# Two attention and expert layers: a head group's products with v issued in one go, filler pieces placed by estimated durations

## The chip, the cores and the metric

One NeuronCore of one Trainium2 chip runs the whole kernel in one launch. The metric is the device time of one execution in microseconds (us); lower is better. Three runs of the kernel before took 1697.82, 1705.48 and 1710.2 us, median 1705.48.

The engines named below are TensorE's matmuls (PE) and weight loads (PEld), VectorE (DVE), ScalarE (ACT), GpSimd (POOL) and SyncE (SP, which issues DMAs). Each engine executes its own instructions in order and waits for others by semaphores.

## The reference

Eight sequences of 512 tokens, 256 wide, pass through two blocks of attention and mixture of experts, all in float32:

```python
x = x + attention0(layernorm(x))   # 16 heads of 16, 4 kv heads, rotary, causal
x = x + ffn0(layernorm(x))         # 32 experts, inner 96, top 8, weights renormalised
x = x + attention1(layernorm(x))   # 16 heads of 16, causal
x = x + ffn1(layernorm(x))         # 16 experts, inner 176, top 2, and a shared FFN of inner 352
```

Attention is `softmax(q k^T / 4) v` under a causal mask, then an output projection. The FFNs are `(silu(x w1) * (x w3)) w2`, weighted by the router's softmax.

## The kernel before

The span has four large stages: attention of layer 0 with routing (30 to 393 us), experts of layer 0 (422 to 884), attention of layer 1 with routing and shared FFN (884 to 1410), experts of layer 1 (1420 to 1657). The change touches the two attention stages.

**One sequence, one group.** `Attention.steps(b)` walks over four head groups c of four heads each. The scores of a group are made transposed, keys on partitions, in three sets n: keys 0 to 127 against all 512 queries (512 wide); keys 128 to 255 and 384 to 511 (384 and 128 wide); keys 256 to 383 (256 wide). `scores` (L638) makes a set as one matmul per head and key block, 32 rows of the array per head, into the PSUM tile `st` (four banks, one buffer). One ACT instruction (L643) takes the exp of a set into `probs`; DVE multiplies the diagonal blocks by the causal mask (L649, 128x512 each, four a group).

`values` (L661) multiplies by v: four key blocks (512, 384, 128, 256 wide) of four heads each, accumulated in the PSUM tile `o` (one bank), 32 output columns of the array per head, with a column of ones that gives the softmax sum. Then DVE copies o to `osb` (L667), PE transposes it (L674, `ot`), and DVE divides by the sum (L677, L678) into `otok`.

**Filler.** `values` is a generator of six pieces. `steps` yields twice per score set, 24 times a sequence, and takes one piece of the preceding group's `values` before each yield. At each yield `pipeline` (L734) also takes pieces of two other generators: `before(b+1)`, which is the norm (`xn_a`), its transposes (`xT_a`, L308) and the q, k and v projections of the next sequence; and `finish(b-1)`, which is the output projection (`oT`, L719; `y`, L727) and `after`, that is the FFN norm (`xn_f`, L292), its transposes (`xT_f`, L308), the router's logits (L321), the choice of experts and the ranks (DVE, and `rk`, L368 and L370), scatters of the rows to DRAM by POOL (L385) and, in layer 1, the shared FFN (`sg`, `su`, L402; silu on ACT, L406; `sy`, L415). Pieces are counted, not weighed: made in equal steps over the sequence, `finish(b-1)` by step 22 of 24 in layer 0 and by the end of the sequence in layer 1. In layer 1 the third generator, `ahead1(b+3)`, gathers a later sequence's x from the experts' outputs (L1200, POOL), from the first step on.

**What sets the order.** The code's order gives priorities; the framework's scheduler then fixes each engine's order from them, from dependencies and from its own cost model. So a piece can be moved away from where the code has it, and a set of four matmuls can be separated by other matmuls. PSUM tiles of all filler pieces come from one ring of three banks (`bank`). `xn_f` has two buffers in layer 0 and one in layer 1; the x tiles form a ring of five.

Of the kernel before, what the change touches and what calls it, by code (L numbers as in the profile page):

```python
# [12 lines left out]
ALU = mybir.AluOpType  # L13
# [59 lines left out]
STEPS = 2 * len(BANKS)  # L73
# [17 lines left out]
def two_blocks_kernel(  # L91
# [78 lines left out]
    def biases1(tmp, bank):  # L170
        wide = tmp.tile([P, ND, P], F32, tag="wide", name="wide", bufs=1)
        lo, _ = BB["o"]
        for m in range(ND):
            nc.vector.tensor_copy(wide[:, m, :], bias1[:, lo + m : lo + m + 1].to_broadcast([P, P]))
        tr = bank("ob")
        for m in range(ND):
            nc.tensor.transpose(tr[:, m * P : (m + 1) * P], wide[:, m, :], ident)
        nc.scalar.copy(ob.rearrange("p m d -> p (m d)"), tr[:, : ND * P])
        yield

        lower = tmp.tile([P, P], F32, tag="lower", name="lower", bufs=1)
        nc.vector.memset(lower[:, :DH], 0.0)
        nc.vector.tensor_copy(lower[:, DH:], ident[:, : P - DH])
        upper_half = tmp.tile([P, 2, 2, 2], F32, tag="upper_half", name="upper_half", bufs=1)
        for n, which in enumerate("qk"):
            lo, hi = BB[which]
            nc.vector.tensor_scalar(
                upper_half[:, :, n, :], bias1[:, lo:hi].rearrange("p (m s) -> p s m", s=2), half[:, 0:1], None, ALU.mult
            )
        both = bank("qkb")[:, :4]  # L190
        for s, turn in enumerate((ident, lower)):
            nc.tensor.matmul(
                both, turn, upper_half[:, s, :, :].rearrange("p n m -> p (n m)"), start=(s == 0), stop=(s == 1)
            )
        nc.vector.tensor_copy(qkb.rearrange("p n m -> p (n m)"), both)
        for s in range(2):
            nc.vector.tensor_scalar(kb[:, :, s], qkb[:, 1, :], half[:, s : s + 1], None, ALU.mult)
        yield
# [98 lines left out]
    def free():  # L297

        for _ in range(4):
            yield  # L300

    def turned(xn, lnp, bank, name):

        xT = lnp.tile([P, ND, T], F32, tag="xT", name=f"xT_{name}")
        for c in range(ND):
            tr = bank(f"xT_{name}_{c}")
            for t in range(NT):
                nc.tensor.transpose(tr[:, t * P : (t + 1) * P], xn[:, t, c * P : (c + 1) * P], ident)  # L308
            nc.scalar.copy(xT[:, c, :], tr)
            yield  # L310
        return xT

    def ffn_parts(smp, bank):
        def route(n, b, xn, xT, name, again):
# [10 lines left out]
            yield  # L325
# [11 lines left out]
            yield  # L337
# [10 lines left out]
            yield  # L348
# [15 lines left out]
            yield  # L364
# [26 lines left out]
            yield  # L391

        def shared(w, xT, x, name):

            hs = smp.tile([P, NS, T], F32, tag="hs", name=f"hs_{name}", bufs=1)
            for n in range(NS):
                rows = min(P, IS1 - n * P)
                g, u = bank(f"sg_{name}_{n}"), bank(f"su_{name}_{n}")
                for o, base in ((g, 0), (u, ND * P)):
                    for c in range(ND):  # L400
                        at = base + c * P
                        nc.tensor.matmul(  # L402
                            o[:rows, :], w[:, n, at : at + rows], xT[:, c, :], start=(c == 0), stop=(c == ND - 1)
                        )
                h = hs[:rows, n, :]
                nc.scalar.activation(h, g[:rows, :], AF.Silu)  # L406
                nc.vector.tensor_tensor(h, h, u[:rows, :], ALU.mult)
                yield
            for half_ in range(NT // 2):
                y = bank(f"sy_{name}_{half_}").rearrange("p (t d) -> p t d", t=2)  # L410
                for i in range(2):
                    t = 2 * half_ + i
                    for n in range(NS):
                        rows = min(P, IS1 - n * P)
                        nc.tensor.matmul(  # L415
                            y[:, i, :], hs[:rows, n, t * P : (t + 1) * P], w[:rows, n, 2 * ND * P :],
                            start=(n == 0), stop=(n == NS - 1),
                        )
                xh = x[:, 2 * half_ : 2 * half_ + 2, :]
                nc.vector.tensor_tensor(xh, xh, y, ALU.add)  # L420
                yield
# [193 lines left out]
    class Attention:  # L615
# [6 lines left out]
        def __init__(self, n, late, ptp, ps, bank, wo, masked=None):  # L622
            self.n, self.fine, self.late, self.ptp, self.ps, self.bank, self.wo = n, fines[n], late, ptp, ps, bank, wo
            self.heads, self.otok, self.rec = {}, {}, {}
            self.last = iter(())
            self.masked = masked

        def scores(self, b, c, n, probs):
# [13 lines left out]
            pt = self.ptp.tile([P, NG, width], F32, tag="p2" if n == 2 else "p01", name=f"p_{name}", bufs=1 + (n < 2))  # L642
# [10 lines left out]
        def values(self, b, c, probs):  # L653
# [4 lines left out]
            for step, j in enumerate((0, 1, 3, 2)):  # L658
# [6 lines left out]
                yield  # L665
            osb = late.tile([P, T], F32, tag="osb", name=f"osb_{name}", bufs=1)
            nc.vector.tensor_copy(osb, o)  # L667
            yield
# [4 lines left out]
            for t in range(NT):  # L673
                nc.tensor.transpose(ot[:, t * P : (t + 1) * P], osb[:, t * P : (t + 1) * P], ident)  # L674
# [7 lines left out]
            yield  # L682

        def steps(self, b):

            for c in range(NCK):  # L690
                probs = {}
                for n in range(len(BANKS)):
                    self.scores(b, c, n, probs)
                    next(self.last, None)
                    yield
                    if n == len(BANKS) - 1:
                        self.last = self.values(b, c, probs)
                    next(self.last, None)
                    yield
                    self.mask(n, probs)  # L700

        def flush(self):
            for _ in range(STEPS - 1):
                next(self.last, None)
                yield

        def output(self, b, x):
# [8 lines left out]
            for k in range(ND):  # L716
# [4 lines left out]
                yield  # L721
            for h in range(NT // 2):
# [9 lines left out]
                yield  # L732

    def pipeline(att, before, after, n_before, n_after, till, ahead=None, lead=0):  # L734
# [9 lines left out]
        n_steps = NCK * STEPS  # L744
        n_after += 4
        drain(before(0))
        for b in range(NB):
            pre = before(b + 1) if b + 1 < NB else iter(())
            post = finish(b - 1) if b else iter(())
            early = ahead(b + 3) if ahead and b + 3 < NB else iter(())  # L750
            made_pre = made_post = 0
            for n, _ in enumerate(att.steps(b)):
                while made_post < n_after * (n + 1 - STEPS) // (till - STEPS):
                    next(post, None)
                    made_post += 1
                while made_pre < n_before * (n + 1 - lead) // (n_steps - 2 - lead):
                    next(pre, None)
                    made_pre += 1
                next(early, None)
            drain(pre)  # L760
            drain(post)
            drain(early)
        drain(att.flush())
        drain(finish(NB - 1))
# [24 lines left out]
    def fast0(awp, lnp, atp, late, ptp, ps, bank):  # L789
# [38 lines left out]
        def before(b):  # L828
# [11 lines left out]
            for t in range(NT):  # L840
# [27 lines left out]
                yield  # L868
            qT = atp.tile([P, 2, T], F32, tag="qT", name=f"qT_{name}")
            for m in range(2):  # L870
# [4 lines left out]
                yield  # L875
# [9 lines left out]
            yield  # L885
# [36 lines left out]
    def fast1(w, v1s, lnp, atp, late, ptp, ps, bank, last):  # L922
# [3 lines left out]
        def before(b):  # L926
# [9 lines left out]
            for h in range(NT // 2):  # L936
# [11 lines left out]
                yield  # L948
            qT = atp.tile([P, 2, T], F32, tag="qT", name=f"qT_{name}")
            kT = atp.tile([P, 2, 2, T], F32, tag="kT", name=f"kT_{name}")  # L950
            for m in range(2):
# [3 lines left out]
                nc.vector.tensor_scalar(qT[:, m, :], q, qkb[:, 0, m : m + 1], None, ALU.add)  # L955
                yield
                kk = bank(f"k_{name}_{m}")
                for k in range(ND):
                    nc.tensor.matmul(kk, w["k"][:, k, m, :], xn[:, k, :], start=(k == 0), stop=(k == ND - 1))
                nc.scalar.activation(  # L960
                    kT[:, m, 0, :], kk, AF.Identity, bias=kb[:, m, 0:1], scale=half[:, 0:1]
                )
                nc.vector.tensor_scalar(
                    kT[:, m, 1, :], kk, half[:, 1:2], kb[:, m, 1:2], ALU.mult, ALU.add
                )
                yield
            att.heads[b] = lambda c: (qT[:, c // 2, :], kT[:, c // 2, c % 2, :], v1, c * NG * (DH + 1))
# [3 lines left out]
    def tables(lay, small, bank, again, beside=None):  # L971
# [10 lines left out]
        yield  # L982
# [10 lines left out]
        yield  # L993
# [4 lines left out]
        yield  # L998
# [5 lines left out]
        yield  # L1004
# [4 lines left out]
        yield  # L1009
# [12 lines left out]
        yield  # L1022

        for lo in range(0, n_e, 8):
# [10 lines left out]
            yield  # L1035
# [206 lines left out]
    def load_x(b, tmp, bank, xf=None):  # L1242
# [3 lines left out]
        for h in range(NT // 2):  # L1246
# [6 lines left out]
            yield  # L1253
# [126 lines left out]
    with ExitStack() as s:  # L1380
# [21 lines left out]
        pipeline(att, before, after0, 15, 12, 22)  # L1402


    with ExitStack() as s1:
# [4 lines left out]
        with ExitStack() as s:  # L1410
# [15 lines left out]
            def after1(b):  # L1426
# [4 lines left out]
                yield from route(1, b, xn, xT, name, False)  # L1431
                yield from shared(w1["s"], xT, xs[b], name)
# [5 lines left out]
            pipeline(att, before, after1, 15, 17, NCK * STEPS, ahead1, 4)  # L1438
# [246 lines left out]
```

## Time and profile before

| | us |
|---|---|
| median of three runs | 1705.48 |
| profiled execution | 1701.29 |
| its span | 1699.6 |
| mean granted TensorE clock | 0.961 |

Starts of the first score set of sequences 0 to 7 in the trace: 30.7, 73.5, 120.0, 164.8, 212.4, 257.8, 307.7, 351.5 in layer 0, and 884.5, 933.1, 996.1, 1059.1, 1122.2, 1191.1, 1261.9, 1324.9 in layer 1.

Three lines of the costliest groups of the page show how it is read: line, engine, operation, tiles and count; then busy time and the mean of one in ns; then the engine's idle time before them and what ended it.

```profile
L638 PE MATMUL st_a<-qT_a,kT_a 32*128 32x512 f32 (+3 forms) x2048 | 202.1, 478 | 11.1 <-ACT p_a L643 10.8
L649 DVE TENSOR_TENSOR p_a<-p_a,causal 128x512 f32<-128x512 f32 x256 | 170.8, 686 | 57.3 <-ACT p_a L643 56.1
L661 PE MATMUL o_a<-p_a,v 128*32 128x512 f32 (+3 forms) x2048 | 197.4, 455 | 6.9 <-DVE p_a L649 6.7
```

A float32 matmul leaves two records, so x2048 are 1024 matmuls: 16 for each of the 64 head groups (8 sequences, 4 groups, 2 layers), four heads in each of four widths. Matmuls of the four heads of a set run side by side in the array, so their busy times overlap, and the distance between starts is the better measure of what a set costs.

### The profile page before, as it was taken

What the parts mean: (1) busy time and instruction counts of PE and PEld (TensorE: products, weight loads), DVE (VectorE), ACT (ScalarE), POOL (GpSimd) and SP (SyncE); (2) the same over time, 40 slices, a digit from 0 to 9 for tenths busy, and PEclk for the clock granted to TensorE, in tenths of its full rate; (3) what the DMA queues carried; (4) which work ended last, traced back from release to release, by engine and by line L of the source; (5) the groups of instructions that cost most, each with busy time, mean ns of one, the idle gap of its engine ahead of it and who ended that gap; (6) DMA issues with size and microseconds to landing.
All of it is one profiled execution on the core that took longest, in us unless ns stands there. A gap on an engine that the chain in (4) does not pass through costs nothing. (4 is left out here: it accounts for less than half of the span.)

```text
span 1699.6 us, 30922 instructions
## 1 busy us (share of the span) xinstructions
PE 1543.7 (91%) x10180; PEld 1029.0 (61%) x10180; DVE 992.0 (58%) x3131; ACT 650.7 (38%) x865; POOL 792.1 (47%) x660
## 2 busy tenths in 40 slices
PE   5899999995999999999989999999899988999982
PEld 2455454543898999998853454544444545777761
DVE  5678887875555555555455764764656544444452
ACT  2555554552233333333334554454355331222221
POOL 0017677577710004888888448888511011000473
PEclk9999999997999999999999999999899998999996
DMA  2035557236988778999995245664312024343563
GB/s 73 13 87 156 163 167 270 102 139 207 307 256 269 202 201 226 266 264 273 268 194 71 39 107 80 127 136 72 86 52 79 26 84 159 109 159 116 156 225 120
DMA packets 255128, 259.43 MB, mean 153 GB/s; under 512 B 80212, under 2 KB 235988, under 8 KB 254964
## 3 DMA queue, kind: packets, MB, share of 16 engines
q1 hardware_dynamic: 199172, 167.88, 32.5%
q0 software_dynamic: 55296, 88.65, 23.0%
q8 instruction: 87, 1.43, 0.4%
q10 hardware_dynamic: 496, 0.85, 0.1%
q14 instruction: 77, 0.63, 0.1%
HBM read 132.70 MB, written 124.57 MB: 151 GB/s over the span
## 5 line engine op out<-in xcount | busy, mean ns | idle before, releaser
L1200 POOL DMA_INDIRECT x_a<-yg,yrows x256 | 402.9, 1574 | 277.2 <-DMA xg_m<-xg 181.9
L385 POOL DMA_INDIRECT xg<-xn_f,rows_f x320 | 321.2, 1004 | 414.7 <-DVE rows_f L382 197.3
L643 ACT ACTIVATE p_a<-st_a 128x2048 f32<-128x2048 f32 (+1 forms) x192 | 306.1, 1594 | 276.4 <-PE st_a L638 243.2
L1131 PE MATMUL gu_m<-gw,xgTs_m 128*128 x1552 | 335.6, 360 | 4.9 <-DVE xgTs_m L1108 3.0
L1131 PEld LDWEIGHTS gu_m<-gw,xgTs_m 128*128 128x128 f32 x1552 | 258.1, 192 | 33.9 <-DVE xgTs_m L1108 3.2
L1162 PE MATMUL y_m<-dw,hTs_m 96*128 (+1 forms) x952 | 237.7, 379 | 0.0
L638 PE MATMUL st_a<-qT_a,kT_a 32*128 32x512 f32 (+3 forms) x2048 | 202.1, 478 | 11.1 <-ACT p_a L643 10.8
L649 DVE TENSOR_TENSOR p_a<-p_a,causal 128x512 f32<-128x512 f32 x256 | 170.8, 686 | 57.3 <-ACT p_a L643 56.1
L661 PE MATMUL o_a<-p_a,v 128*32 128x512 f32 (+3 forms) x2048 | 197.4, 455 | 6.9 <-DVE p_a L649 6.7
L1108 DVE COPY xgTs_m<-xgT_m 128x512 f32<-128x512 f32 x194 | 133.9, 690 | 109.7 <-PE xgT_m L1106 109.4
L1167 ACT COPY ys_m<-y_m 128x512 f32<-128x512 f32 x194 | 113.7, 586 | 189.1 <-PE y_m L1162 174.7
L1123 DVE SCALAR_TENSOR_TENSOR h_m<-h_m,xg_m,gu_m 128x96 f32<-128x96 f32 (+1 forms) x388 | 114.8, 326 | 115.2 <-ACT h_m L1136 69.3
L1162 PEld LDWEIGHTS y_m<-dw,hTs_m 96*128 96x128 f32 (+1 forms) x952 | 165.3, 190 | 15.1
L1262 POOL DMA_INDIRECT g<-yg,yrows x64 | 65.2, 1018 | 202.2 <-DVE h_m L1123 170.9
L638 PEld LDWEIGHTS st_a<-qT_a,kT_a 32*128 32x128 f32 x2048 | 90.1, 189 | 107.2 <-issue 52.4
L1152 DVE COPY hTs_m<-hT_m 96x256 f32<-96x256 f32 (+1 forms) x194 | 92.7, 478 | 99.5 <-PE hT_m L1151 98.5
L1106 PE MATMUL xgT_m<-ident,xg_m 128*128 128x128 f32 x776 | 119.3, 275 | 16.0 <-DMA xg_m<-xg 13.2
L1139 ACT ACTIVATE h_m<-gu_m 128x192 f32<-128x192 f32 x150 | 49.7, 331 | 212.2 <-PE gu_m L1131 200.6
L1106 PEld LDWEIGHTS xgT_m<-ident,xg_m 128*128 128x128 f32 x776 | 95.6, 141 | 39.2 <-issue 16.6
L661 PEld LDWEIGHTS o_a<-p_a,v 128*32 128x32 f32 x2048 | 49.3, 110 | 107.8 <-issue 66.1
L1151 PE MATMUL hT_m<-ident,h_m 128*96 128x128 f32 (+1 forms) x476 | 84.9, 274 | 0.6 <-DVE h_m L1123 0.4
L667 DVE COPY osb_a<-o_a 128x512 f32<-128x512 f32 x64 | 44.0, 688 | 53.0 <-PE o_a L661 53.0
(198 smaller groups left out, 1689.6 us busy)
## 6 DMA issues: line engine op xcount, KB each, us to landing
yg<-ys_m SPq DMA_DIRECT2D x194, 256.0 KB
xg_m<-xg SPq DMA_DIRECT2D x300, 144.0 KB
xg_m<-xg SPq DMA_DIRECT2D x88, 136.0 KB
xg<-zeros SPq DMA_DIRECT2D x66, 144.0 KB
xg<-xn_f,rows_f POOLq DMA_INDIRECT x320
xg<-zeros SPq DMA_DIRECT2D x34, 136.0 KB
xf<-in_x_dram SPq DMA_DIRECT2D x8, 512.0 KB
x_after<-x_in SPq DMA_DIRECT2D x8, 512.0 KB
```

The source lines that it names most:

```text
L385: inst = nc.gpsimd.indirect_dma_start(out=lay.xg, out_offset=bass.IndirectOffsetOnAxis(ap=rows[:, t, i : i + 1], axis=0), in_=xn[:, t, :], ...
L638: nc.tensor.matmul(st[:, g, at : at + T - j * P], kT[r, j * P : (j + 1) * P], qT[r, j * P :], start=True, stop=True,)
L643: nc.scalar.activation(pt, st[:, :, :width], AF.Exp, scale=SCALE)
L649: self.masked = nc.vector.tensor_tensor(d, d, causal.unsqueeze(1).to_broadcast([P, NG, P]), ALU.mult).ins
L661: nc.tensor.matmul(o[32 * g : 32 * g + 32, j * P :], v1[:, j, v_at + g * (DH + 1) :][:, :32], probs[n][:, g, at : at + T - j * P], start=( ...
L1106: nc.tensor.transpose(tr[:, j, c, :], xg[:, j, c * P : (c + 1) * P], ident)
L1108: nc.vector.tensor_copy(xT, tr)
L1123: nc.vector.scalar_tensor_tensor(h[:, j, :], h[:, j, :], xg[:, j, D:][:, bass.ds(offs[part, i + j][2], 1)], gus[j][:, inner:], ALU.mult, A ...
L1131: nc.tensor.matmul(gus[j], xT[:, j, c, :], gu[:, bass.ds(at + c * 2 * inner, 2 * inner)], start=(c == 0), stop=(c == ND - 1),)
L1162: nc.tensor.matmul(y[:, j, :], hT[:n_in, q, j, :], dn[:n_in, bass.ds(at + q * D, D)], start=(q == 0), stop=(q == n_ch - 1),)
L1167: nc.scalar.copy(ys, y)
L1200: nc.gpsimd.indirect_dma_start(out=xs[b][:, t, :], out_offset=None, in_=yg, in_offset=rows, compute_op=ALU.add)
```

## The change

1. `values` becomes two functions: `products`, all 16 matmuls and the copy to `osb` with no yield between, and `normalize`, the transposes and the division. `products` is called right behind the next group's first scores, `normalize` behind the second, nothing behind the third. The copy moves from DVE to ACT.
2. `steps` yields once per score set: 12 gaps a sequence.
3. The probabilities of sets 0 and 1 get three buffers instead of two.
4. Pieces yield an estimated duration in us; a negative one is a wait, after which no further piece of that generator is taken while it is ahead of its share. Class `Fill` holds a generator, its total, and its share of each of the three kinds of gap. `pipeline` takes pieces from the generator that is furthest behind its share, until none is behind and a least amount (`LEAST`) is filled. `finish(b-1)` now runs from the third gap of sequence b to the second gap of sequence b+1.
5. In layer 1 the router's and the shared FFN's pieces alternate, and q and k are put into tiles of one half each with three buffers. Gathers are issued twice per gap from the third gap on.

The new `with ExitStack():` in `pipeline` holds nothing; the order is the scheduler's, as before.

```diff
+NGAP = NCK * len(BANKS)
+LEAST = (0.0, 1.6, 1.2)
@@ scores
-            ... bufs=1 + (n < 2))
+            ... bufs=3 if n < 2 else 1)
@@ values
-        def values(self, b, c, probs):
+        def products(self, b, c, probs):
...
-                yield
-            osb = late.tile([P, T], F32, tag="osb", name=f"osb_{name}", bufs=1)
-            nc.vector.tensor_copy(osb, o)
-            yield
+            self.osb = late.tile([P, T], F32, tag="osb", name=f"osb_{name}", bufs=1)
+            nc.scalar.copy(self.osb, o)
+
+        def normalize(self, b, c, probs):
...
@@ steps
-                    next(self.last, None)
-                    yield
-                    if n == len(BANKS) - 1:
-                        self.last = self.values(b, c, probs)
-                    next(self.last, None)
+                    if self.last:
+                        (self.products, self.normalize, lambda *_: None)[n](*self.last)
                     yield
                     self.mask(n, probs)
+                self.last = (b, c, probs)
@@ pipeline
+    class Fill:
+        def __init__(self, part, total, share, first, last):
+            self.part, self.total, self.first, self.last = part, total, first, last
+            whole = sum(share[k % len(BANKS)] for k in range(first, last + 1))
+            self.share = [total * s / whole for s in share]
+            self.gap = -1
+            self.at = self.due = 0.0
+            self.waits = False
+        def pass_gap(self, n):
+            self.gap += 1
+            if self.gap >= self.first:
+                self.due += self.share[n]
+        def behind(self):
+            return (self.due - self.at) / self.total
+        def able(self):
+            return self.part and self.gap >= self.first and (self.behind() > 0.0 or not self.waits)
+        def make(self):
+            cost = next(self.part, None)
...
+            self.waits = cost < 0.0
+            self.at += abs(cost)
+            return max(cost, 0.0)
...
+            for b in range(NB):
+                if b:
+                    last = NGAP + 1 if b + 1 < NB else NGAP - 1
+                    fills.append(Fill(finish(b - 1), t_after(b - 1), share, 2, last))
+                if b + 1 < NB:
+                    fills.append(Fill(before(b + 1), t_before, share, 0, NGAP - 2))
...
+                    while True:
+                        able = [f for f in fills if f.able()]
+                        if not able:
+                            break
+                        fill = max(able, key=lambda f: f.behind())
+                        if fill.behind() <= 0.0 and filled >= LEAST[k % len(BANKS)]:
+                            break
+                        filled += fill.make()
+                    for fill in [f for f in fills if f.gap > f.last]:
+                        drain(fill.part)
+                        fills.remove(fill)
+                    if k > 1:
+                        next(early, None)
+                        next(early, None)
@@ after0, after1
-        pipeline(att, before, after0, 15, 12, 22)
+        pipeline(att, before, after0, 12.7, lambda b: 13.5 + ..., (0.05, 0.55, 0.4))
-                yield from route(1, b, xn, xT, name, False)
-                yield from shared(w1["s"], xT, xs[b], name)
+                routed, beside = route(1, b, xn, xT, name, False), shared(w1["s"], xT, xs[b], name)
+                for made in (routed, beside, routed, routed, beside, routed, routed):
+                    yield next(made)
+                drain(routed)
+                yield from beside
-            pipeline(att, before, after1, 15, 17, NCK * STEPS, ahead1, 4)
+            pipeline(att, before, after1, 15.1, lambda b: 29.2 + ..., (0.25, 0.42, 0.33), ahead1)
```

The remaining lines of the diff put numbers into `yield`: 0.5 for a set of four transposes, 1.4 for a token tile's q, k and v, 1.75 for a half of a projection, 1.9 for the logits, 3.5 for a piece of the shared FFN's gate and up, 2.6 for half of its output, and waits of -0.4 to -1.0.

## The prediction

> **What bounds the kernel now.** I read the page first, then the busy time by stage, then groups by shape, then the waits, then the timeline of a few places.
>
> ```profile
> PE 1543.7 (91%) x10180; PEld 1029.0 (61%) x10180; DVE 992.0 (58%) x3131; ACT 650.7 (38%) x865; POOL 792.1 (47%) x660
> 30.00:393.00 363.00, 336.65 (x2887) 171.51 (x2885) 279.15 (x1001) 196.23 (x183) 193.11 (x191) 0.98 0.41 133
> 884.00:1410.00 526.00, 485.08 (x3257) 249.40 (x3256) 304.89 (x997) 242.51 (x216) 271.61 (x191) 0.96 0.39 80
> ```
>
> The first line is the whole run, the other two the attention of layer 0 and of layer 1 (length; busy PE, PEld, DVE, ACT, POOL; clock). PE is busy 93% and 92% of them, so only 26.4 + 40.9 = 67.3 us can be won by filling PE; anything more must be cheaper PE work. DVE is at 77% in layer 0, and works in order. The expert stages are not touched.
>
> ```profile
> L661 PE MATMUL o_a<-p_a,v 128*32 128x512 f32 x512 | 82.2, 626 | 2.7 <-DVE p_a L649 2.7
> L643 ACT ACTIVATE p_a<-st_a 128x2048 f32<-128x2048 f32 x128 | 240.5, 1879 | 241.8 <-PE st_a L638 211.9 <-issue 7.6 <-PE rk_f L370 3.2
> L667 DVE COPY osb_a<-o_a x64: 677/691/693, 44.3 to 1386.0; 128x512 f32<-128x512 f32 x64
> PE xT_f L308 <- DVE xn_f L292: 30.1, 11, 6.2
> PE xT_a L308 <- DVE xn_a L292: 10.2, 3, 4.7
> ```
>
> The score tile st has one buffer, so a group of four heads runs scores, exp, scores, exp, scores, exp, with 1.88 us for a large exp. The shortest distances between the starts of score sets are 3.14, 3.19 and 2.20 us behind the first, second and third set, 8.5 us a group and 34 a sequence. A sequence takes 43 to 50 us in layer 0 and 63 to 71 in layer 1. So a gap between score sets lasts as long as the larger of its PE work and that chain. I price PE work by the distances of dense starts: a set of four heads takes 1.07 (scores 512 wide), 1.08 (384 and 128), 0.64 (256); products 1.00, 0.67, 0.33, 0.57 for 512, 384, 128, 256; four transposes 0.5; one token tile's projection 1.43.
>
> Check on the old order, sequences 1 to 6, whose gaps I summed from the trace. Layer 0: 42.0 + 42.1 + 43.6 + 41.8 + 47.2 + 43.1 = 259.8, against 278.0 measured (73.5 to 351.5); 18.2 is left for waits. Layer 1: 58.8 + 4x59.9 + 60.0 = 358.4, against 391.8 (933.1 to 1324.9); 33.4 is left.
>
> ```profile
> 174.13 0.30 PE L719 MATMUL oT_a<-ident,otok_a 128*128 128x128 f32 x1 [2.23 <-DVE otok_a L678]
> 175.15 1.02 ACT L643 ACTIVATE p_a<-st_a 128x1024 f32<-128x1024 f32 x1 [2.61 <-PE st_a L638]
> 1149.95 1.38 DVE L292 TENSOR_SCALAR xn_f<-x_a,mv_f,rstd_f 128x256 f32<-128x256 f32 x4 [4.11 <-DMA xg<-xn_f,rows_f]
> ```
>
> Here the waits are. PE stands at the output transposes for DVE's otok, so the third scores and their exp are late: about 2.2 us in each sequence of layer 0. In layer 1 the FFN norm waits for the scatter that reads the old xn_f; that costs sequences 4 and 5 some 7 us each.
>
> **The change, part by part.** *Products in one go.* No matmul goes away. In the changed instruction order, products follow products 169 times instead of 63, and PE switches between scores, products and other matmuls 520 times instead of 663. A set of products is 0.1 us shorter behind products (0.9 against 1.00), so some 0.8 us a sequence.
>
> *Sets torn apart.* The order is still the scheduler's, and it tears more four-head sets than before:
>
> ```profile
> 160.66 1.04 PE L661 MATMUL o_a<-p_a,v 128*32 128x512 f32 x2
> 161.63 0.66 PE L879 MATMUL kT_a<-ident,kr_a 128*128 128x128 f32 x4
> 163.79 1.06 PE L661 MATMUL o_a<-p_a,v 128*32 128x512 f32 x8
> 164.78 1.14 PE L638 MATMUL st_a<-qT_a,kT_a 32*128 32x512 f32 x8
> ```
>
> (A matmul is two records.) One head alone holds PE for 161.63 - 160.66 = 0.97 us, and the remaining heads hold it another 0.99: a torn set costs nearly double. The new order tears 20 sets of 512-wide products against 11, 10 of 256-wide scores (25 pieces) against none, 8 of 512-wide scores (18 pieces) against 3 (7): by the prices above some 39 us of repeated work against 15, over both layers. What of it is paid depends on the gap it falls into.
>
> *Gaps.* I summed the new order in the same way. In sequence 3 of layer 0 the first gap holds 2.06 us of PE work, below the 3.14 of its chain; the gaps behind the second and third scores of the second group hold 5.18 and 5.24, with the 256-wide scores torn. Sequences 1 to 6: 47.0 + 45.5 + 47.5 + 46.1 + 52.5 + 46.7 = 285.3; less 6x0.8 for adjacent products, less 4x0.67 where a torn 384 piece runs beside three 512 ones: 277.8. Waits come on top. The 2.2 us at the output transposes go (finish now starts behind the third scores), 13 of the 18.2; what is late next is a 512-wide product pulled ahead of the 256-wide scores, which waits for DVE's masks, with scores, exp and all later PE work behind it, and DVE's xn_a, just in time for xT_a. I take 8 us of waits, between 0 (all covered) and 18.2 (as before): 285.8, so **+8 us**, from 0 to +18. Sequences 0 and 7 give **+1**.
>
> *Layer 1.* The same sum: 56.4 + 4x59.6 + 64.2 = 359.0, less 4.8 for adjacent products: 354, 4 less than before. It is not won, because of POOL. The gathers of a sequence's x (32 at 1.87 us, 60 us) wait for a ring slot that frees when sequence 0's finish is done, and alternate with scatters of 10.5 us; the chain from 1004 to 1218.5 sets xn_f in sequences 4 and 5. In the new order finish ends in the next sequence's second gap, so the slot frees a little later: the scatter that frees xn_f ends some 335.5 us into layer 1 instead of 334. I take **+2 us**, from -15 (half of the 33.4 of waits gone) to +10 (finish work of 4.6 us pushed past a boundary twice, at the end of the stage too). The split qT and kT only add buffers, and their copies are as many as before: nothing, as their waits are not among the long ones.
>
> *osb copied by ACT.* 64 copies of 0.69 leave DVE, 2.75 us a sequence; ACT gets 64 of about 0.59 (its other 512-wide copies), behind an exp and before the next scores have finished, ACT being idle for almost half the stage. I give it nothing; without that cover it is 64 x 0.59 = 38 us. The third buffer of the probabilities lets exp run before the products have read the old one; it costs nothing.
>
> *Silu placed in three gaps.* Route and shared FFN are interleaved, so exp and silu alternate in three gaps a sequence, not two.
>
> ```profile
> 1108.40 1.88 ACT L643 ACTIVATE p_a<-st_a 128x2048 f32<-128x2048 f32 x1
> 1110.30 1.28 ACT L406 ACT_TABLE_LOAD   x1
> 1111.59 0.60 ACT L406 ACTIVATE hs_f<-sg_f 128x512 f32<-128x512 f32 x1
> ```
>
> A load takes 1.28 us and nothing around it. The three gaps hold 6.90, 5.84 and 5.30 us of PE work; their chains with a load in each are 3.19 + 1.28 = 4.47, 3.48 and 4.47, so all is hidden. [...]
>
> In all 8 + 1 + 2 = **+11 us**, against the profiled run's 1701.3 (span 1699.6): 1712. The median of the runs is 4 us above it, so the forecast is **1716**.
>
> **Rivals.** *Waits gone (faster).* The pieces fill PE where it stood: the waits of layer 0 vanish (0 instead of 8), torn pieces fall into idle time (half of the 24 us more), and layer 1 gains 15 us because scatters come early enough. 1705 + 0 + 1 - 12 - 15 = about 1680. For it: the 67 us of PE idle time; against it: gaps below 2.7 us of work beside gaps above 5 us in the new order.
>
> *DVE in order (slower).* With products early, the masks of a set decide PE's next piece. DVE, 77% busy, has xn_a's, rank and route steps ahead of them; 2.5 us more per sequence, twelve sequences, is 30 us: 1716 + 30 = 1746. It decides once a mask reaches PE later than the chain allows, that is over 0.3 us behind the exp.
>
> *POOL sets layer 1.* Layer 1 is fixed whatever PE does, and only layer 0 counts: +8 or so, 1714. This is inside my forecast's own case.
>
> *Nothing changes.* The scheduler undoes the placing, and the time is that of before: 1705.
>
> **Numbers.** About 1% (17 us) is what can be told from no change. Forecast with POOL's case, 0.50 (own range 1700 to 1732); faster, 0.20; DVE in order, 0.22; nothing changes, 0.08. The unknown waits carry part of the forecast's case over 1722. So faster 0.19, within 1% 0.44, slower 0.37. The range 1690 to 1746 leaves out the outer half of each far case.
>
> **What would show it.** In the changed profile PE busy time in layer 0 should be up by 10 to 20 us with the same matmuls; lone 512-wide products of about 1 us should be seen; the wait of oT for otok should be gone, and PE's wait for masks be longer; table loads should be above 15 pairs, with no longer exp waits behind them. I am wrong if PE's idle time in layer 1 falls by more than 15 us, or if torn sets overlap with what follows them.

## The result and the profile after

The changed kernel takes 1721.02 us (median of nine runs, 1712.07 to 1727.41), the kernel before 1703.35 on the same chip. The ratio is 1.0095, with an interval of 1.0073 to 1.0117: slower by 1%. The prediction had 1716 and a range of 1690 to 1746. The spans of the two profiles differ by 1717.6 - 1699.6 = 18.0 us.

From the first scores to the end of the last products, layer 0 takes 376.0 us instead of 361.5 (+14.5) and layer 1 506.1 instead of 501.4 (+4.7). What lies between them grows by 2.7, and the rest of the kernel shrinks by 3.9. First the page's busy times, then the two stages (their own lengths, so the bounds differ from those of before).

```profile
PE 1565.6 (91%) x10180; PEld 1060.9 (62%) x10180; DVE 958.0 (56%) x3067; ACT 702.6 (41%) x943; POOL 787.5 (46%) x660
```

```profile
30.00:407.00 377.00, 349.59 (x2884) 188.02 (x2883) 262.48 (x967) 211.93 (x214) 187.82 (x186) 0.96 0.39 127
901.00:1408.00 507.00, 477.67 (x3191) 252.80 (x3190) 271.79 (x876) 274.52 (x256) 267.51 (x190) 0.95 0.38 78
```

PE is busy 22 us longer with the same 10180 matmul records, DVE 34 us less. The number after POOL's is the granted clock. The waits of PE and two groups by shape answer to those shown before:

```profile
PE st_a L642 <- ACT p_a L647: 23.0, 24, 2.0
...
PE xT_f L311 <- DVE xn_f L293: 20.7, 17, 5.3
...
PE xT_a L311 <- DVE xn_a L293: 11.9, 3, 6.5
PE oT_a L722 <- DVE x_a L424: 7.4, 5, 1.5
...
PE o_a L665 <- DVE p_a L653: 2.9, 2, 2.7
```

```profile
L665 PE MATMUL o_a<-p_a,v 128*32 128x512 f32 x512 | 93.1, 630 | 2.7 <-DVE p_a L653 2.7
```

```profile
L647 ACT ACTIVATE p_a<-st_a 128x2048 f32<-128x2048 f32 x128 | 240.3, 1877 | 194.8 <-PE st_a L642 193.9 <-DVE w_a L277 0.9
L670 ACT COPY osb_a<-o_a 128x512 f32<-128x512 f32 x64 | 37.4, 584 | 26.0 <-PE o_a L665 25.0 <-ACT p_a L647 0.5 <-PE cps L1030 0.5
L647 ACT ACT_TABLE_LOAD x22 | 28.2, 1283 | 2.8 <-PE st_a L642 2.4
```

In layer 0 the output transposes no longer wait; in layer 1, where they hardly waited before, they do (7.4 us for x). PE waits for exp 23.0 us instead of 10.8 (the gaps with less work than their chain), and its wait for the masks fell from 6.7 to 2.9, though the prediction expected more. Table loads are 22 pairs instead of 15, and the wait with them fell from 14.6 to 2.4 us.

The sums of the prediction can be set against the times. For sequences 1 to 6, the larger of PE work and chain in each gap, summed without the corrections for adjacent products, and the time in the trace; the rest is the time less the sum (every torn filler piece is priced with a start of its own here, which makes these sums 2 to 4 us larger than the prediction's):

| | layer 0: sum, time, rest | layer 1: sum, time, rest |
|---|---|---|
| before | 263.7, 278.0, 14.3 | 360.9, 391.7, 30.8 |
| changed | 289.5, 293.0, 3.6 | 362.1, 407.8, 45.7 |

By these sums layer 0 lost by what the order makes PE do in each gap, and layer 1 by what the sums leave out. That is not longer waiting: PE stands idle for 27.4 us of layer 0's stage (377.00 - 349.59) against 26.4 before, and for 29.3 us of layer 1's against 32.2 (502.0 us from 884 to 1386, 469.8 busy). In good part it is time at half clock, as the second table behind e12 shows. A stretch of the timeline in layer 0, and the clock in it:

```profile
204.11 1.04 PE L311 MATMUL xT_f<-ident,xn_f 128*128 128x128 f32 x8
205.08 1.05 PE L665 MATMUL o_a<-p_a,v 128*32 128x512 f32 x2
206.05 0.69 PE L642 MATMUL st_a<-qT_a,kT_a 32*128 32x256 f32 x2
206.68 0.41 PE L325 MATMUL lg_f<-rw,xT_f 128*128 128x32 f32 x2
207.02 0.69 PE L642 MATMUL st_a<-qT_a,kT_a 32*128 32x256 f32 x2
207.64 1.98 PE L325 MATMUL lg_f<-rw,xT_f 128*128 128x32 f32 x14
209.55 1.23 PE L642 MATMUL st_a<-qT_a,kT_a 32*128 32x256 f32 x4
210.70 3.63 PE L665 MATMUL o_a<-p_a,v 128*32 128x512 f32 x22
```

```profile
206.00:208.00 2.00, 2.00 (x11) 1.24 (x10) 0.96 (x2) 0.60 (x2) 1.49 (x2) 1.00 0.24 78
208.00:210.00 2.00, 2.00 (x15) 1.94 (x16) 0.31 (x2) 0.00 (x0) 1.60 (x2) 0.75 0.43 145
210.00:212.00 2.00, 2.00 (x12) 0.61 (x14) 1.59 (x15) 1.33 (x2) 1.39 (x3) 0.50 0.23 76
```

One head of a 512-wide product holds PE from 205.08 to 206.05, 0.97 us as priced. The 256-wide scores are torn into three pieces around the logits, and the last begins 3.5 us after the first. And something the prediction did not see: PE is busy without a break from 198.2 on, yet at 209 the clock falls to half, and products that take 2.36 us elsewhere (32 records) take 3.63 for 22. The same happens at 116.9, 359.2 and 1376.4 (no break since 104.9, 348.6 and 1372.7), each time behind the router's logits and one-head scores.

In layer 1 ten of the eleven stretches at half clock begin between 0.1 us before and 2.3 us after the end of a wait of PE of 0.3 to 2.5 us. One of them: the first two lines are DVE's, the others PE's:

```profile
1079.37 0.42 DVE L684 TENSOR_TENSOR otok_a<-ot_a,rec_a 128x256 f32<-128x256 f32 x1
...
1081.31 0.68 DVE L424 TENSOR_TENSOR x_a<-x_a,sy_f 128x512 f32<-128x512 f32 x1
...
1082.05 0.66 PE L722 MATMUL oT_a<-ident,otok_a 128*128 128x128 f32 x4 [1.47 <-DVE x_a L424]
...
1085.38 3.62 PE L731 MATMUL y_a<-wo,oT_a 128*128 128x256 f32 x8
...
1094.45 1.89 PE L731 MATMUL y_a<-wo,oT_a 128*128 128x256 f32 x8
```

```profile
1084.00:1086.00 2.00, 2.00 (x7) 1.44 (x7) 0.00 (x0) 0.38 (x1) 1.70 (x2) 0.50 0.80 113
```

PE waits 1.47 us. It is not for otok, which is ready at 1079.8, but for the end, at 1082.0, of DVE's addition of the shared FFN's output of the sequence before last (L424, pushed past the boundary). The addition is the last to read one of the three filler banks, and the transposes need one; that this is the link is read from the code. Then the clock is half for 6.8 us, and the same output projection takes 3.62 us instead of 1.89.

### The profile page after: what moved, and what is told of

It is laid out like the page before. It is cut to its first block, busy times and chain, and to the rows that moved or that the text cites. A ratio compares the mean times of both kernels' runs of the same rounds, so it can differ in the third digit from the quotient of the medians.

```text
span 1717.6 us, 30921 instructions
## 1 busy us (share of the span) xinstructions
PE 1565.6 (91%) x10180; PEld 1060.9 (62%) x10180; DVE 958.0 (56%) x3067; ACT 702.6 (41%) x943; POOL 787.5 (46%) x660
## 5 line engine op out<-in xcount | busy, mean ns | idle before, releaser
L642 PE MATMUL st_a<-qT_a,kT_a 32*128 32x512 f32 (+3 forms) x2048 | 221.4, 479 | 23.4 <-ACT p_a L647 23.0
L665 PE MATMUL o_a<-p_a,v 128*32 128x128 f32 (+3 forms) x2048 | 189.0, 451 | 3.1 <-DVE p_a L653 2.9
L642 PEld LDWEIGHTS st_a<-qT_a,kT_a 32*128 32x128 f32 x2048 | 96.2, 189 | 144.9 <-ACT p_a L647 61.9
L665 PEld LDWEIGHTS o_a<-p_a,v 128*32 128x32 f32 x2048 | 63.0, 111 | 118.7 <-issue 100.4
L1200 PEld LDWEIGHTS hT_m<-ident,h_m 128*96 128x96 f32 (+1 forms) x476 | 58.4, 125 | 19.5 <-issue 7.4
## 6 DMA issues: line engine op xcount, KB each, us to landing
yg<-ys_m SPq DMA_DIRECT2D x194, 256.0 KB
```

The source lines that it names most:

```text
L642: nc.tensor.matmul(st[:, g, at : at + T - j * P], kT[r, j * P : (j + 1) * P], qT[r, j * P :], start=True, stop=True,)
L665: nc.tensor.matmul(o[32 * g : 32 * g + 32, j * P :], v1[:, j, v_at + g * (DH + 1) :][:, :32], probs[n][:, g, at : at + T - j * P], start=( ...
L1200: nc.tensor.transpose(hp[:n_in, q, j, :], h[:, j, lo : lo + n_in], ident)
```

## The experiments

Theory A: the loss is the order that the scheduler gives PE (torn sets, pulled-ahead pieces, and the low clock behind them). Rival B: it is the new placing of the filler (shares by gap, finish across the boundary, router and shared FFN alternating). e1 to e8 ran on a second chip, e9 to e12 on a third. On both the kernel before takes 2024 to 2027 us, because in layer 0 all engines pause while POOL scatters (shown under e1 for the second chip), so times are compared with each other, not with 1703. The changed kernel itself, with its scatters, has no time on these two chips.

**e1 and e5: PE in the code's order.**

```diff
-        with ExitStack():
+        with tc.manual_schedule(engines={ENG.PE}):
             drain(before(0))
```

> The changed kernel with PE's order in the two attention stages as the code has it; the other engines stay with the scheduler. No set is torn then (0 instead of 49), and no product or filler piece is pulled ahead of the next scores. Theory A (the loss is the scheduler's PE order: torn sets, and waits behind pulled-ahead pieces that also halve PE's clock): summed as in the prediction, sequences 1 to 6 of layer 0 come to 265 us instead of 289 and of layer 1 to 356 instead of 362, so 30 us less, with fewer stretches of low clock: 1680 to 1695 us. Rival B (the loss is the new placing itself: finish across the boundary, silu in three gaps, osb on ACT): these stay, and PE can no longer step round a wait: 1715 to 1730.

Measured: 2047.45 us, before 2024.35, ratio 1.0097 (1.0066 to 1.0128). The pauses hide the question. In the waits and the timeline of this kernel ("remote" is said where the profile finds nothing in the program that ended a wait):

```profile
ACT p_a L647 <- remote: 164.9, 10, 32.0
```

```profile
205.49 1.33 PE L642 MATMUL st_a<-qT_a,kT_a 32*128 32x384 f32 x15
...
207.28 0.36 PE L642 MATMUL st_a<-qT_a,kT_a 32*128 32x128 f32 x1 [0.46 <-issue]
...
229.22 1.88 ACT L647 ACTIVATE p_a<-st_a 128x2048 f32<-128x2048 f32 x1 [14.87 <-issue]
```

The scores are done at 207.6 and the exp begins at 229.2. All that ACT does between is one copy of 0.59 us, at 213.8, which was late itself. POOL scatters from 201.6 to 241.9. In the DMA records the transfers of instructions stop at 203.8 and go on at 241.7; on the first chip they arrive during such a burst (16 KB each at 211.6, 228.9 and 243.3 in the kernel before, whose scatters run from 209.2 to 251.5).

> The kernel of e1 once more, since on e1's chip all kernels lost some 300 us in layer 0 to pauses of every engine during POOL's scatters, which hide the question. On a chip without these pauses (before near 1705 us) the expectation of e1 stands: Theory A 1680 to 1695 us, rival B 1715 to 1730. With the pauses, the ratio to before says nothing on A and B, and only gaps of layer 1 outside POOL's bursts can be compared.

Measured: 2048.88 us, ratio 1.0116 (1.007 to 1.0162). The pauses were there again: a repeat that settled nothing.

**e2: sets made indivisible.** A critical section around each loop over the four heads, in `scores` and `products`.

```diff
-                for g in range(NG):
+                with tc.tile_critical():
+                    for g in range(NG):
```

> The changed kernel with each set of four matmuls of scores and of products made one indivisible section, everything else left to the scheduler. Theory A, tearing alone: sums of 274 instead of 289 us for sequences 1 to 6 of layer 0, about the same in layer 1; 1700 to 1710 if the sections cost nothing themselves (their own instructions may cost some 0.05 us each, 512 of them, which the trace will show). Rival B: 1721 or more.

Measured: 3303.85 us, ratio 1.63 (1.626 to 1.634). The 0.05 us for a section was a guess that no run shows; the sections cost far more. In the timeline of layer 0:

```profile
133.75 2.09 PE L643 MATMUL st_a<-qT_a,kT_a 32*128 32x512 f32 x8 [2.30 <-DVE p_a L654]
```

From 120 to 140 us each set stands behind 1.2 to 2.4 us of waiting, and the clock is low (0.69 in the mean of the run). It says nothing on tearing.

**e3: osb copied by DVE.**

```diff
-            nc.scalar.copy(self.osb, o)
+            nc.vector.tensor_copy(self.osb, o)
```

> The changed kernel with the copy to osb back on DVE; tears 48 sets instead of 49. Theory A: no change beyond some us either way, as ACT's copy lies in its idle time: 1716 to 1726. Rival B with ACT as the culprit (the copy delays exp): 64 x 0.59 = 38 us less at most, 1685 to 1710. Rival with DVE as the culprit in the old kernel: DVE takes 44 us more, 1730 or more.

Measured: 2056.08 us, ratio to before 1.0139 (1.0105 to 1.0173). The two are compared where no pause falls, in sequences 0 and 1 of layer 0: 94.8 us here, 90.1 in the changed kernel's profile on the first chip. With DVE's copy the group's transposes wait 5.8 us for it in sequence 1. So ACT's copy is no cost; it saves 4.7 us in this one stretch.

**e4: the kernel before, PE in its code's order.** The same line of manual schedule around the body of its `pipeline`.

> The kernel before with PE's order in the two attention stages as its code has it. It tears no set (18 before), but each piece stands where it was counted, so PE stands at pieces that are not ready. The sums are 262 instead of 264 us for sequences 1 to 6 of layer 0 and 369 instead of 361 in layer 1, so without waits 1708. Theory A expects waits on top (pieces placed by count): 1710 to 1760, and that the changed placing in code order (e1) beats it by 15 us or more. Rival B: e1 is no faster than this one.

Measured: 2026.72 us, ratio 0.9993 (0.9966 to 1.002). So the scheduler's order of PE is no better than the code's for this kernel, and e1, 20 us slower, does not beat it: against theory A, as far as kernels with pauses can show it.

**e6: products in one go, alone.** The kernel before with `values` cut as in the change, and its filler pieces counted as before:

```diff
+            yield
...
             for step, j in enumerate((0, 1, 3, 2)):
...
-                yield
...
-            nc.vector.tensor_copy(osb, o)
+            nc.scalar.copy(osb, o)
+            yield
             yield
             if c == 0:
```

Three buffers for the probabilities and q and k in half tiles go with it.

> The kernel before with one part of the change alone: products in one go behind the next group's first scores, osb copied by ACT, normalize behind the second, three buffers for the probabilities, and q and k in half tiles (for the space). Filler pieces are counted as before. Its PE order tears 22 sets of 512-wide products (11 before). Sums of sequences 1 to 6: 279 instead of 264 us in layer 0, 370 instead of 361 in layer 1, less 10 for adjacent products. Theory A (torn sets and gaps shorter than their chain): 1710 to 1725 against 1705. Rival B (the loss is the placing of the pieces, finish across the boundary and silu in three gaps): 1695 to 1706.

Measured: 1988.09 us, before 2026.62, ratio 0.9808 (0.9772 to 0.9845): faster by 1.9%, outside both expectations. Nothing is left out in it, and it beats the kernel before on this chip.

**e7: finish ends in its own sequence.**

```diff
-                    last = NGAP + 1 if b + 1 < NB else NGAP - 1
+                    last = NGAP - 1
```

> The changed kernel with finish(b-1) ending with sequence b, not in the second gap of b+1. Its order tears 66 sets instead of 49. Sums of sequences 1 to 6: 288 instead of 289 us in layer 0, 374 instead of 362 in layer 1; against that, in layer 1 the output transposes no longer wait for DVE's additions of the shared FFN (some 20 us with the low clock that follows). Theory A: 1710 to 1730. Rival B with the boundary as the culprit: 1695 to 1706.

Measured: 2044.23 us, ratio 1.0092 (1.0061 to 1.0124). So it is still slower than the kernel before without the work past the boundary: either the boundary alone is not the cause, or what this gains goes into the 66 torn sets (49 in the changed kernel).

**e8: shared FFN behind the router.** `yield from route(...)` and then `yield from shared(...)`, as in the kernel before.

> The changed kernel with the shared FFN of layer 1 behind the router's pieces, as in the kernel before, so exp and silu alternate in fewer gaps. Sums 364 instead of 362 us in layer 1, 57 torn sets instead of 49. Theory A and the prediction's reading of the table loads (1.28 us each, hidden): 1718 to 1728. [...]

Measured: 2026.63 us, ratio 0.9994 (0.9971 to 1.0018), some 18 us faster than e7, and the only variant of the changed kernel that takes no longer than the kernel before on this chip. But its profile still has 22 pairs of table loads, so it does not test what they cost. The gain is that of another order, and what in it was not settled.

**e9 to e12: without layer 0's scatters and gathers.** To have no pauses, these four leave out POOL's scatters of layer 0; two direct DMAs write rows of the same tile to fixed places. The gathers that add the experts' rows to x are left out too. The orders of PE are those of the kernels they come from.

```diff
+            if n == 0 and not again:
+                slabs = lay.xg[: n_e * lay.cap, :].rearrange("(e r) w -> r e w", e=n_e)
+                at = (b - lay.seqs[0]) * 192
+                for t, rows_ in ((0, P), (1, 64)):
+                    nc.sync.dma_start(out=slabs[at + t * P : at + t * P + rows_, :, :],
+                        in_=xn[:rows_, t, :].unsqueeze(1).to_broadcast([rows_, n_e, lay.width]))
             for t in range(NT):
-                for i in range(k):
+                for i in range(k if n or again else 0):
```

> The kernel before without POOL's scatters and gathers of layer 0: the 32 scatters of a sequence are replaced by two direct DMAs on SP that write the same rows to fixed places, and x of layer 1 gets no sum of experts' rows. PE's order is that of the kernel before. Pause theory (instruction transfers do not arrive while POOL issues indirect DMAs without a break): no pauses of all engines in layer 0, which takes 362 us from the first scores to the last products, within 5, as in the first profile (361.5). If the pauses have another cause they stay, and layer 0 takes over 550 us. Layer 1 loses the waits for the late scatters: 480 to 490 us instead of 501.

> The changed kernel, with the same left out; PE's order is that of the changed kernel. If the loss of layer 0 comes from PE's order (torn sets, short gaps, low clock), it is there without scatters: 376 us within 4, some 14 more than e9. If POOL's scatters or what waits for them made it, layer 0 is within 4 us of e9. In layer 1 POOL's chain is gone: by the sums 362 against 361 us, equal to e9 within 6 if the sums rule, 10 to 20 us longer if the low clock behind the output transposes' waits does.

> The changed kernel with PE's order as the code has it (that of e1), and the same left out. Theory A: no torn set, sums of 265 us instead of 289 for sequences 1 to 6 of layer 0 (264 in the kernel before), 356 instead of 362 in layer 1: layer 0 takes 345 to 356 us, under e9 and 20 or more under e10. Rival B (placing): PE stands at pieces that are not ready, 365 us or more, and over e10 in layer 1.

> The kernel of e6 (products in one go, nothing else), with the same left out. Sums of 279 us for sequences 1 to 6 of layer 0, 15 more than e9: 365 to 375 us in layer 0 by them. In layer 1 e6 had few stretches of low clock (12 us lost against 17 in the first profile) and 490 us in all: 475 to 485 here. If torn sets are what costs, it lies between e9 and e10 in layer 0; if the pieces' placing is, it equals e9 there.

Measured, on one chip in the same rounds (medians), with the lengths of the attention stages in the profiles:

| | us | layer 0 | layer 1 | sum, time, rest of layer 0 | of layer 1 |
|---|---|---|---|---|---|
| e9 before | 1760.56 | 362.3 | 502.6 | 263.7, 279.2, 15.5 | 360.9, 391.0, 30.1 |
| e10 changed | 1800.17 | 374.0 | 522.6 | 289.5, 289.8, 0.3 | 362.1, 414.6, 52.5 |
| e11 changed, PE in code order | 1789.47 | 371.1 | 520.1 | 265.2, 282.1, 17.0 | 355.8, 409.0, 53.2 |
| e12 products in one go alone | 1728.65 | 351.8 | 475.2 | 279.0, 271.2, -7.8 | 369.6, 372.3, 2.7 |

The stages by busy time, the first line of each kernel for layer 0 and the second for layer 1; the third number from the end is the clock. e9:

```profile
30.00:394.00 364.00, 338.47 (x2889) 172.47 (x2887) 277.57 (x1001) 196.31 (x183) 0.00 (x0) 0.98 0.63 181
918.00:1422.00 504.00, 471.15 (x3193) 235.40 (x3191) 291.12 (x933) 238.03 (x210) 54.44 (x56) 0.97 0.13 42
```

e10:

```profile
31.00:406.00 375.00, 348.14 (x2884) 187.63 (x2883) 261.04 (x968) 212.12 (x214) 0.00 (x0) 0.96 0.59 168
941.00:1464.00 523.00, 485.32 (x3191) 258.77 (x3190) 271.67 (x876) 272.99 (x256) 55.03 (x56) 0.94 0.13 41
```

e11:

```profile
30.00:402.00 372.00, 330.03 (x2888) 181.57 (x2888) 263.00 (x976) 213.03 (x215) 0.00 (x0) 0.91 0.60 173
933.00:1454.00 521.00, 475.32 (x3192) 255.08 (x3190) 271.71 (x876) 273.25 (x256) 55.51 (x56) 0.94 0.13 41
```

e12:

```profile
30.00:383.00 353.00, 329.99 (x2887) 177.89 (x2885) 262.97 (x976) 211.49 (x215) 0.00 (x0) 0.99 0.64 185
913.00:1389.00 476.00, 453.56 (x3192) 240.88 (x3190) 275.25 (x901) 255.08 (x242) 54.69 (x56) 0.99 0.14 45
```

The pauses are gone with the scatters: layer 0 takes 362.3 us, as on the first chip (361.5). That missing instruction transfers are the link, as the pause theory has it, is inferred from their times in e1. The loss of layer 0 is there without them too, 374.0 - 362.3 = 11.7, so it is not POOL's. Three expectations were missed. Layer 1 of e9 did not get shorter than the first profile's 501 us: most of its sequences take 64.5 us instead of 63. Layer 1 of e11 is not longer than that of e10, as rival B had it. And layer 0 of e12 takes 351.8 us where 365 to 375 were expected by the sums, and rival B had it equal to e9.

In layer 1 each of the four has 24 to 31 us of waits, mostly of ACT and DVE, that the profile calls remote, as in the pauses; the first chip's two profiles have none there, and layer 0 of the four has none. So layer 0 is the cleaner comparison.

A time below the sum, as e12 has, shows that the prices are too high for its order. So the sum is made once more, with PE's work read from the trace: its busy time in each gap, less half of what ran at half clock. The rest is the time above it. "Lost" is the full speed lost to the half clock, half the length of its stretches, and the most that it can have cost (the projection above took 3.62 us in such a stretch and 1.89 behind it).

| sequences 1 to 6, us | layer 0: sum, rest, lost | layer 1: sum, rest, lost |
|---|---|---|
| before, first chip | 263.8, 14.3, 3.4 | 370.3, 21.5, 8.5 |
| changed, first chip | 276.3, 16.7, 11.4 | 363.0, 44.7, 23.9 |
| e9 before | 263.8, 15.4, 5.1 | 372.3, 18.7, 3.4 |
| e10 changed | 275.8, 14.0, 9.3 | 369.1, 45.5, 22.1 |
| e11 changed, PE in code order | 256.0, 26.2, 17.8 | 363.7, 45.2, 20.5 |
| e12 products in one go alone | 270.7, 0.5, 0.0 | 366.0, 6.3, 3.4 |

So of the 15.0 us that layer 0 lost on the first chip, 12.5 are the sum's and up to 8.0 the half clock's, while other waits fell. Layer 1's sum fell by 7.3 and its rest grew by 23.2, up to 15.4 of it by the half clock.

Theory A falls as the whole cause. With no set torn (e11), PE is busy 18 us less in layer 0 than in e10, but the stage is only 3 us shorter and longer than e9: PE now stands at pieces that are not ready (idle 42.0 us instead of 26.9), and the clock is 0.91. And e12, which tears 32 sets, is the fastest of the four in both layers. Rival B stands in the main: one part of the change, products in one go with the copy on ACT, gains 10.5 us in layer 0 and 27.4 in layer 1 (e12 against e9); the new placing, which is all that the change does besides, takes 22.2 and 47.4 back (e10 against e12). With scatters the gain of the first part is seen too (e6). Which part of the placing does it was not isolated: moving finish back (e7) did not help by itself; the kernel without the alternation (e8) came back to the time of before, but the changed kernel has no time beside it.

## Why the prediction was right

The total was right (1716 against 1721, +11 against +18), but in part by luck. Sequences 1 to 6, which the sums are about, lost 15.0 us in layer 0 and 16.0 in layer 1, three times the 8 + 2 that were forecast; all the rest of the kernel gained 13 us, 10.0 of them in sequence 0 of layer 1, which no step foresaw. Of its steps, some held and some only came out.

*Layer 0, +8, from 0 to +18.* Measured +15.0 (278.0 to 293.0). By the prediction's own sum of 277.8 this leaves 15.2 us where 8 were taken. That the order makes PE's gaps longer held: by the sum from the trace they grow by 12.5 us, where the prediction had 18. The waits that were to go were smaller than it read: PE stood at layer 0's output transposes for 8.0 us in five waits, not 13. What it named as late next, DVE's masks, was wrong (2.9 us over the whole run). In its place came waits of up to 2 us for exp (16.9 us in the stage instead of 4.8) and a term that the prediction put at nothing, the half clock: over the whole stage it lost 15.4 us of full speed, against 6.8 before. Three of its six stretches follow no wait (no gap of PE in the 10.6 to 11.9 us before them) but one-head scores and logits.

*Torn sets.* The price was right (0.97 us again). That e10's layer 0, 289.8 us, meets the sum of 289.5 is chance: this sum lacks the 7.5 us of corrections that the prediction made, and up to 9.3 us of the time are lost to the clock. Tearing is not a cause that stands alone; taken away, other waits take its place (e11).

*Products in one go, 0.8 us a sequence.* This step failed most. It took the part only for the shorter distance of adjacent products. e12 shows that it also removes most of what lies above the sum (by the trace 0.5 and 6.3 us are left of 15.4 and 18.7), though the sum of layer 0 grows by 7. The copy leaves DVE, the normalisation comes a full set earlier than the transposes that need it, PE stands less (idle 23.0 us of the stage instead of 25.5, and 22.4 instead of 32.9 in layer 1), and in layer 0 the clock does not fall in these sequences (0.0 us lost). That the last two follow from the first two is argued, not shown; the third buffers and the half tiles came with it.

*Layer 1, +2 by POOL's chain.* Measured +4.7, for another reason and by luck: sequences 1 to 6 take 16.0 us more and sequence 0 takes 10.0 less (38.7 instead of 48.7). The scatter that frees xn_f does end 336.5 us into the layer, where the prediction had 335.5, but the FFN norm waits for it 2.2 us instead of 9.5, so POOL did not set the layer. The 4 us less in the sum were there (7 by the trace). What the step left out is the clock: PE waits at the FFN norm's and output transposes, all six of its waits at the latter, of 1.5 to 2.1 us, are followed by half clock 0.25 to 2.34 us later, and sequences 1 to 6 lose 23.9 us of full speed, against 8.5. In e10 against e9, where layer 0's scatters and gathers are left out, the difference is +20.0, not a gain, with the remote waits in it. The rival that POOL sets layer 1 falls too.

*osb on ACT, nothing.* It is a gain in the one stretch that can be compared (e3). *Table loads.* 22 pairs, hidden, as read: the exp of 1.88 us, the load of 1.28 and the silu in the trace before left 0.03 us between them, and 36 of the 46 loads in the changed kernel have their next instruction 0.01 us behind them. What a load costs beyond its 1.28 us was not tested apart; e8 has 22 pairs too.

## What to carry to other kernels

Sum, for each gap of a pipeline, the larger of the bound engine's work and the chain that runs through it, from the instruction order and the trace's own distances. Here it gave the direction of the work (+18 forecast, +12.5 found in layer 0), not what waits and the half clock add. Test the parts of a large change one at a time; here a part worth -2% (e12 against e9) and a part worth +4% (e10 against e12) went in together. And look at the clock behind a wait of one or two us on TensorE: behind the wait of 1.47 us at 1080.6 came 6.83 us at half clock, up to 3.4 us of full speed. Of the 16 gaps of 1.4 us or more in the changed kernel's two stages, nine had a stretch at half clock of 3.41 or 6.83 us begin in them (two) or 0.25 to 2.34 us behind them (seven).

## What the runs showed of the hardware

**The clock fell behind short waits, and without any.** In the changed kernel's two attention stages the 17 stretches at half clock last 3.41 or 6.83 us each; in the kernel before two last 10.24 and 13.65. One began 0.8 us after a wait of 1.47 us had ended (1082.8 in the changed kernel). Another, at 209.0, followed 10.9 us in which PE's records leave no gap: behind one-head scores and 32-wide logits. Four of the 17 began behind such sets; why is not shown.

**No instruction transfer arrived in a burst of POOL's scatters on the second chip.** In the DMA records of e1 no 16 KB or 8 KB transfer of instructions arrived between 203.8 and 241.7 us, while POOL issued 32 scatters with 0.30 us between one and the next, and ACT, DVE and PE stood idle for up to 14.87, 32.41 and 21.65 us. That the engines stood for want of instructions is inferred from these times. Without layer 0's scatters the pauses were gone (e9, layer 0 in 362.3 us, on the third chip, where the kernel before is as slow: 2027.17 against 2024.35). On the first chip neither the kernel before nor the changed one shows any: PE's longest idle time in layer 0 is 2.66 and 2.65 us, and instructions arrive during the scatters (211.6, 228.9 and 243.3 in the kernel before). Why the chips differ stays open.
